# An attention and mixture-of-experts kernel: the first batch's experts computed per chosen pair instead of densely

## The chip, the cores and the metric

The kernel runs as one program on one core of a Trainium2 chip. The time is device time in microseconds (us) of one execution, and a kernel's time is the median of its runs. The engines are called as the profile calls them: PE is TensorE (matrix products), PEld its loads of weights, DVE is VectorE, ACT is ScalarE, POOL is GpSimd, SP is SyncE, which here only starts transfers (DMAs). Each engine works through its own queue of instructions in order, and waits where an operand is not there yet.

## The reference

The input is x, two batches of 1024 tokens of 256 numbers, in float32. A first attention layer with one head (queries, keys and values of 256) is added to x and normalised. A block follows: a layer norm, a causal attention with 16 heads of 128 with rotary embedding, a residual, and a mixture of four experts behind a second layer norm, of which each token uses two:

```python
raw = jax.nn.softmax(x @ w_gate, axis=-1)                  # x: 2048 tokens x 256, 4 experts
top_vals, top_idx = jax.lax.top_k(raw, TOP_K)              # TOP_K = 2
w = jax.nn.softmax(top_vals, axis=-1)
comb = jnp.zeros((t, E), x.dtype).at[jnp.arange(t)[:, None], top_idx].add(w)
hmid = jax.nn.gelu(jnp.einsum('td,edi->tei', x, we1) + be1[None], approximate=False)
eout = jnp.einsum('tei,eid->ted', hmid, we2) + be2[None]   # we1, we2: 4 x 256 x 256
out = jnp.einsum('te,ted->td', comb, eout)
```

The experts' output is added to the block's residual, and a last normalisation gives the result. The reference computes every expert for every token and multiplies by `comb`, in which two of the four weights of each token are zero.

## The kernel before

**Tiles.** A row tile is 128 tokens on the 128 partitions; a batch has eight (`NT`), J0 is tiles 0 to 3 and J1 tiles 4 to 7. An attention row (`RowA`, `RowB`) is the work of one head on one row tile: scores on PE, a mask and row maximum on DVE, an exponential on ACT, a normalisation, a transposition of the probabilities, the product with the values (av), and the output product. For some rows the probabilities are transposed in blocks by DVE and put together by SyncE transfers (`gather`, the pT copies, line 702), for others by PE. There are 272 rows: 16 of the first attention, then 256 of the second in 32 units of eight rows, a unit being one head of one batch. Row `s` = 256 begins the last two units; the loop over rows ends at 272.

**Order.** Nothing is left to a scheduler. `do(f, ...)` writes a named operation down; `at`, `first`, `mid`, `end_of` and `late` attach one to a row's step; `step(t)` writes down the parts of the rows that are under way and what is attached. The list `MOVES` then takes single operations to behind another one, by name, and `ordered` gives the final order in which all of them are issued:

```python
    for f in ordered(ops, MOVES):
        f()
```

**The experts before.** `m_stats`, `m_rstd`, `m_norm` make the second layer norm (`m_norm` of batch 0 on GpSimd, of batch 1 on VectorE, one instruction for a row tile), `m_transposed` (line 524 by its helper) turns it, `gate_products` and `gate_logits` (1626, 1642) make the logits, `gate`, `gate_best`, `gate_weights` (1664 to 1708) find each token's two experts and weights on VectorE with two exponentials on ACT. `m_bias` (1715) adds the weighted second bias. `hidden(b, j, e)` (1728, 1736) is four products of 512 columns for one expert and four tiles, evacuated by ACT with the Gelu; `expert(b, j, slots)` (1751, 1760) is the second product of 256 columns, added with its weight to `h`, the residual, by VectorE. So each batch runs eight hiddens and eight sets of expert products. `m_residual` (1611) adds the residual with accumulating transfers of GpSimd, `o_stats` and `o_finish` make the last normalisation and store it. `load_experts` (1538 to 1544) loads `we1` and `w_gate`; `load_second` (1548 to 1550) `we2` and its bias. Exponential, square root and Gelu need different function tables on ACT; `table()` puts a load of the table in front where the last one was of the Gelu.

Batch 0's layer norm, gate and first two hiddens lie among the last 16 rows. After row 271 come batch 0's other experts, with batch 1's residual, norm and gate between them, and then batch 1's experts:

```python
    do(m_rstd, 1, J0)
    do(m_bias, 0, (3,))
    do(all_of, 0, 0, 1)
    do(m_norm, 1, 0)
```

`all_of(b, j, e)` is `expert` for one expert and four tiles. Products are collected in PSUM: scores in `ps_sc` (two), transposes in `ps_tr` (two), hiddens in `acc_tile()` (two of 512 columns). `rope_sb` holds the rotary tables, last used by the last rotation; `lent` is two tiles that the first attention's weights leave to `we2`; x1 is the first attention's output, held in SBUF until it is stored.

## Time and profile before

| what | value |
|---|---|
| median of three runs | 1139.58 us (1139.5 to 1141.21) |
| the profiled execution's own time | 1144.33 us |
| its span, first to last instruction | 1141.7 us |
| granted PE clock over the span | 0.998 |
| bytes moved by DMA | 133.89 MB, 117 GB/s on average |
| of these from and to device memory | 22.71 MB read, 4.19 MB written |

The profile records one execution. Its page gives each engine's busy time, the chain of work that ended last, and groups of instructions by line and shape. In the trace, one row stands for neighbouring instructions of one kind: start, duration, engine, line, operation, out<-in, shapes and number, and in square brackets how long the engine waited before it and for what. A row of a stretch gives the stretch, its duration, the busy time and number of instructions of PE, PEld, DVE, ACT and POOL, the granted PE clock, the share of DMA time and GB/s. Matrix products in float32 appear as two records each. GpSimd's last rotation ends at 957.9, and the last PE instruction at 1136.0.

### The profile page before, as it was taken

What the parts mean: (1) busy time and instruction counts of PE and PEld (TensorE: products, weight loads), DVE (VectorE), ACT (ScalarE), POOL (GpSimd) and SP (SyncE); (2) the same over time, 40 slices, a digit from 0 to 9 for tenths busy, and PEclk for the clock granted to TensorE, in tenths of its full rate; (3) what the DMA queues carried; (4) which work ended last, traced back from release to release, by engine and by line L of the source; (5) the groups of instructions that cost most, each with busy time, mean ns of one, the idle gap of its engine ahead of it and who ended that gap; (6) DMA issues with size and microseconds to landing.
All of it is one profiled execution on the core that took longest, in us unless ns stands there. A gap on an engine that the chain in (4) does not pass through costs nothing.

```text
span 1141.7 us, 15909 instructions
## 1 busy us (share of the span) xinstructions
PE 1125.4 (99%) x4616; PEld 714.3 (63%) x4616; DVE 782.5 (69%) x1809; ACT 651.9 (57%) x1228; POOL 784.3 (69%) x736
## 2 busy tenths in 40 slices
PE   9999989999999999999999999999999999999998
PEld 6666645656565656565757575757575657566665
DVE  5557776858585867676767676676767678576575
ACT  3333576665656565656565656565656556553444
POOL 4005999999998989697869777888889999000000
PEclk9999999999999999999999999999999999999999
DMA  6132475666556454555555545555555576414311
GB/s 190 38 87 59 118 175 131 154 137 128 127 119 132 114 139 111 120 119 131 118 125 134 126 111 130 129 139 128 135 135 134 125 156 160 108 43 91 58 38 37
DMA packets 243453, 133.89 MB, mean 117 GB/s; under 512 B 18884, under 2 KB 241160, under 8 KB 242856
## 3 DMA queue, kind: packets, MB, share of 16 engines
q1 hardware_dynamic: 238352, 121.45, 46.1%
q0 software_dynamic: 2288, 6.98, 2.7%
q10 hardware_dynamic: 2728, 4.46, 1.1%
q8 instruction: 37, 0.61, 0.2%
q14 instruction: 48, 0.39, 0.1%
HBM read 22.71 MB, written 4.19 MB: 24 GB/s over the span
## 4 chain that ended last, share of the span: by engine, by line
PE 90%; POOL 5%; DVE 2%; ACT 1%; SPq 1%; DMA 1%; issue 0%; ACTq 0%; POOLq 0%; DVEq 0%
PE av L1240 21%; PE sc L1174 20%; PE pa L950 10%; PE pa L941 6%; PE pa L1098 5%; PE pa L1728 5%; PE pe L1751 4%; PE pc L950 4%; PE sc L721 2%; PE pc L1098 2%; PE pc L941 2%; POOL rot L863 2%; PE pa L770 2%; PE pa L611 1%; PE pa L624 1%; PE pa L1050 1%
## 5 line engine op out<-in xcount | busy, mean ns | idle before, releaser
L1191 ACT ACTIVATE pr<-pr,rs 128x128 f32<-128x128 f32 (+3 forms) x252 | 196.0, 779 | 190.5 <-DVE rs L1189 190.3
L643 DVE CUSTOM_DVE_ANT_0 sc<-sc,mask 128x640 f32<-128x640 f32 (+7 forms) x272 | 206.4, 759 | 128.2 <-PE sc L1174 113.5
L1174 PE MATMUL sc<-Twk,Twq 128*128 128x512 f32 (+3 forms) x768 | 289.5, 487 | 2.8 <-ACT pr L651 1.9
L1240 PE MATMUL av<-pT,vg 128*128 128x512 f32 (+3 forms) x768 | 270.0, 489 | 3.6 <-DMA pT<-pair_sb 3.3
L651 ACT ACTIVATE pr<-sc,nmx 128x640 f32<-128x640 f32 (+7 forms) x272 | 201.2, 740 | 114.0 <-DVE nmx L643 86.6
L1240 PEld LDWEIGHTS av<-pT,vg 128*128 128x128 f32 x768 | 143.7, 191 | 127.5 <-issue 100.1
L863 POOL TENSOR_TENSOR rot<-Twk,rope_sb 64x512 f32<-64x512 f32 x128 | 166.5, 1301 | 79.1 <-DVE Twk L983 57.5
L1174 PEld LDWEIGHTS sc<-Twk,Twq 128*128 128x128 f32 x768 | 135.6, 191 | 123.0 <-issue 104.0
L863 POOL TENSOR_TENSOR rot<-Twq,rope_sb 64x512 f32<-64x512 f32 x128 | 169.1, 1321 | 8.8
L691 DVE STREAM_TRANSPOSE x<-pr 128x640 f32<-128x640 f32 (+1 forms) x124 | 128.6, 1038 | 20.4 <-ACT pr L1191 17.7
L865 POOL TENSOR_TENSOR Twk<-Twk,rot 128x512 f32<-128x512 f32 x64 | 87.0, 1359 | 5.0
L864 POOL TENSOR_TENSOR Twk<-Twk,rope_sb 128x512 f32<-128x512 f32 x64 | 85.6, 1337 | 5.0
L864 POOL TENSOR_TENSOR Twq<-Twq,rope_sb 128x512 f32<-128x512 f32 x64 | 82.4, 1288 | 5.0
L865 POOL TENSOR_TENSOR Twq<-Twq,rot 128x512 f32<-128x512 f32 x64 | 82.1, 1283 | 5.0
L691 DVE STREAM_TRANSPOSE pair_sb<-pr 128x128 f32<-128x128 f32 (+1 forms) x120 | 60.5, 504 | 11.6 <-ACT pr L1191 11.5
L1611 POOL DMA_DIRECT2D hx<-x_dram x4 | 3.5, 1145 | 91.5 <-DVE hx L1715 82.4
L1107 DVE TENSOR_TENSOR hx<-hx,pa 128x512 f32<-128x512 f32 x70 | 48.0, 686 | 22.2 <-PE pa L1098 21.2
L1256 ACT ACTIVATE aT_sb<-av,par 128x512 f32<-128x512 f32 x64 | 43.9, 687 | 30.9 <-PE av L1240 26.3
L1728 PE MATMUL pa<-xT,we_flat 128*128 128x512 f32 x128 | 57.5, 593 | 0.0
L1751 PE MATMUL pe<-lent,hT 128*128 128x256 f32 x240 | 54.4, 379 | 0.0
L651 ACT ACTIVATION_READ_ACCUMULATOR pr<-sc,nmx 128x1 f32 x272 | 53.4, 196 | 0.0
L1751 PEld LDWEIGHTS pe<-lent,hT 128*128 128x128 f32 x240 | 45.4, 190 | 9.5 <-issue 3.1
(221 smaller groups left out, 1794.6 us busy)
## 6 DMA issues: line engine op xcount, KB each, us to landing
pT<-x SPq DMA_DIRECT2D x496, 128.0 KB, 2.7
pT<-pair_sb SPq DMA_DIRECT2D x480, 64.0 KB, 2.0
pT<-aT_sb SPq DMA_DIRECT2D x48, 128.0 KB, 2.6
pT<-za SPq DMA_DIRECT2D x48, 64.0 KB, 2.0
wk_g<-in_L_ffn_wk_dram SPq DMA_DIRECT2D x9, 256.0 KB, 3.0
wq_g<-in_L_ffn_wq_dram SPq DMA_DIRECT2D x9, 256.0 KB, 3.1
wv_g<-in_L_ffn_wv_dram SPq DMA_DIRECT2D x9, 256.0 KB, 3.0
wo_g<-in_L_ffn_wo_dram SPq DMA_DIRECT2D x9, 256.0 KB, 2.9
```

Of the source, the lines that this page charges most:

```text
L643: nc.vector.tensor_tensor_reduce(out=sc[:, :L], in0=sc[:, :L], in1=mask[:, S - L :], scale=-1.0, scalar=BIG, op0=ALU.add, op1=ALU.min, acc ...
L651: nc.scalar.activation(pr[:, :L], sc[:, :L], AF.Exp, bias=nmx, scale=-1.0, accum_out=sm)
L691: nc.vector.transpose(z[:, i % 4, :n, :], pr[:, : n * 32].rearrange("p (m s) -> p m s", s=32))
L863: nc.gpsimd.tensor_tensor(rot[lo, :], t[hi, cs], rope_sb[hi, 1, cs], ALU.mult)
L864: eng.tensor_tensor(t[:, cs], t[:, cs], rope_sb[:, 0, cs], ALU.mult)
L865: nc.gpsimd.tensor_tensor(t[:, cs], t[:, cs], rot, ALU.add)
L950: nc.tensor.matmul(pa, lhsT=w, rhs=x, start=start, stop=True, skip_group_check=True)
L1174: nc.tensor.matmul(sc[:, ds(n0, n)], lhsT=qT[:, ts(i, P)], rhs=kT[:, ds(n0, n)], start=True, stop=True,)
L1191: nc.scalar.activation(self.pr[:, :L], self.pr[:, :L], AF.Copy, scale=rs)
L1240: nc.tensor.matmul(cut(av), lhsT=vg[g, b][:, c, ts(hh, HD)], rhs=cut(pT[:, c, :]), start=(c == 0), stop=(c == i),)
L1728: nc.tensor.matmul(ph, lhsT=we1_sb[:, e, c, ts(m, P)], rhs=x2T[:, c, ds(k0 * P, 512)], start=(c == 0), stop=(c == DC - 1),)
L1751: nc.tensor.matmul(pe[:, ts(n, D)], lhsT=hTs[b, j, e][:, c, ts(k, P)], rhs=we2_sb[e][:, c, :], start=(c == 0), stop=(c == IC - 1),)
```

## The change

Batch 0's eight hiddens and eight sets of expert products are taken out. In their place:

- The gate is made some rows earlier, and `m_norm` of batch 0 moves from GpSimd to VectorE. `ws` keeps the two weights of each token.
- Each (token, expert) pair chosen gets a slot. Slots are grouped by expert, each expert beginning a new tile of 128; with 2 x 8 tiles of pairs and at most three more for the rounding up, there are `NS` = 19 slot tiles. `sparse_counts` counts tokens per expert by two products with constant matrices; `sparse_slots` turns the counts into each pair's slot (`place_ids`) and each slot tile's expert (`expert_ids`). Constants and small tables lie in the rotary table's space, written by `sparse_constants` after the last rotation.
- `sparse_scatter` writes each normalised row to its two slots in device memory (`slot_x`), with 16 indirect DMAs of GpSimd, a memset behind each. `slot_x` is filled with zeros by seven DMAs on SyncE near the start. `sparse_load` reads the slots back, four tiles a DMA.
- Per slot tile, `sparse_transposed`, `sparse_hidden` and `sparse_out` compute one expert: w1 is copied within SBUF by SyncE from an address in a register (`sparse_weights`), w2 is read by PE at an address in a register, and each register is loaded from `expert_ids` (`sparse_ids`). Results go to `slot_y` in device memory, two tiles a store.
- `sparse_gather` reads both results of each token back into x1's space with 16 indirect DMAs of GpSimd, and `sparse_add` adds them with their weights on VectorE, 16 instructions.
- `PLACES` attaches the first part to the last 16 rows; `queue` and `MORE` set how many slot operations stand between the parts of batch 1's work after row 271. Batch 1's experts stay dense. Of `MOVES`, 49 entries at the end of the list go and seven come.

```diff
--- before.py
+++ after.py
 MOVES = (
     ("m_rstd 1 7", "o_finish 1 1 2"),
-    ("o_finish 1 1 1", "o_stats 1 1 2"),
...
-    ("m_stats 0 0.1.2.3", "load_experts"),
+    ("o_finish 1 1 1", "expert 1 1 3.3"),
+    ("o_finish 1 1 0", "expert 1 1 3.2"),
+    ("hidden 1 1 2", "o_finish 0 1 0.1.2.3"),
+    ("hidden 1 0 2", "sparse_add 0 3"),
+    ("RowB.transpose 271", "b_output 7 1 2.3"),
+    ("RowB.scores 266", "RowB.gather 263 0"),
+    ("b_output 6 1 3", "RowB.transpose 263"),
     ("load_weights 6 wo #2", "RowB.normalise 254"),
...
+    lent_flat = const.tile([P, B * 3 * 512], F32, name="lent")
+    lent = [lent_flat[:, ts(b, 3 * 512)] for b in range(B)]
...
+    NS = 2 * NT + E - 1
+    slot_x = dpool.tile([NS * P, D], F32, name="slot_x")
+    slot_y = dpool.tile([NS * P, D], F32, name="slot_y")
...
+    for k in range(0, NS, 3):
+        n = min(3, NS - k)
+        nc.sync.dma_start(
+            slot_x[ds(k * P, n * P), :].rearrange("(n p) d -> p n d", p=P),
+            mask[:, : n * D].rearrange("p (n d) -> p n d", d=D),
+        )
...
-                nc.vector if b else nc.gpsimd,
+                nc.vector,
...
+    def sparse_constants():
+        g = nc.gpsimd
+        g.memset(ones, 1.0)
+        g.memset(before, 1.0)
+        g.affine_select(
+            out=before, in_=before, compare_op=ALU.is_ge, fill=0.0, base=-1,
+            pattern=[[1, P]], channel_multiplier=-1,
+        )
+        for k in range(NT):
+            g.memset(limits[:, :, k : k + 1], float(k * P))
+        for n in range(NS):
+            g.memset(starts[:, n, :], float(n * P))
+        for t in steps_of:
+            g.memset(t[:, :NT, :], 0.0)
+        g.memset(steps_of[0][:, NT : NT + 1, :], 0.0)
+        g.memset(tiles_of[:, 0, :], 0.0)
+        g.memset(marks[:, :, 0:1], 1.0)
+        g.memset(marks[:, :, E : E + 1], 0.0)
...
+    def sparse_counts(b):
+        nc.vector.tensor_tensor(picked, found[b, 0][1], found[b, 1][1], ALU.add)
+        pc = ps_tr.tile([P, 512], F32, tag="tr", name="pc")
+        flat = picked.rearrange("p t e -> p (t e)")
+        for k, lhsT in enumerate((ones, before)):
+            nc.tensor.matmul(
+                pc[:, ts(k, NT * E)], lhsT=lhsT, rhs=flat, start=True, stop=True
+            )
+        counts[b] = pc
+    def sparse_slots(b):
...
+        v.tensor_copy(place_ids, places)
+        v.tensor_tensor(
+            marks[:, :, 1:E], starts,
+            bases[:, 1:].unsqueeze(1).to_broadcast([P, NS, E - 1]), ALU.is_ge,
+        )
+        v.tensor_reduce(experts_of, marks[:, :, 1:E], AX.X, ALU.add)
+        v.tensor_copy(expert_ids, experts_of)
...
+    def sparse_scatter(b, t):
+        for n in range(2):
+            put = nc.gpsimd.indirect_dma_start(
+                out=slot_x, out_offset=at_row(n, t),
+                in_=xn2[b, t // 4][:, t % 4, :], in_offset=None,
+            )
+            tc.declare_no_dep(put.ins, group="slots", reason="each slot is of one token and choice")
+            tc.add_to_no_dep_group("slots", put.ins)
+            puts.append(put.ins)
+            nc.gpsimd.memset(ones[:, 0:1], 1.0)
+    def sparse_ids(engine, lo, hi):
+        _, vals = nc.values_load_multi_w_load_instructions(
+            expert_ids[0:1, lo:hi], engines=[engine], min_val=0, max_val=E - 1,
...
+    def sparse_load(k):
+        n = min(4, NS - 4 * k)
+        tag = ("Twk", "Twk", "Twq")[k % 3]
+        t = bpool.tile([P, 4, D], F32, tag=tag, name="xs", bufs=BUFS[tag[1:]])
+        nc.sync.dma_start(
+            t[:, :n, :], slot_x[ds(4 * k * P, n * P), :].rearrange("(n p) d -> p n d", p=P)
+        )
+    we1_rows = we1_flat.rearrange("p (e x) -> p e x", e=E)
+    we2_rows = lent_flat[:, : E * IC * D].rearrange("p (e x) -> p e x", e=E)
+    def sparse_weights(s):
+        t = wpool.tile([P, DC, I], F32, tag=("wq", "wk", "wv")[s % 3], name="w1")
+        nc.sync.dma_start(
+            t.rearrange("p c i -> p (c i)"),
+            we1_rows[:, ds(sp_ids[s], 1), :].rearrange("p a x -> p (a x)"),
+        )
+    def sparse_transposed(q):
+        n = min(2, NS - 2 * q)
+        pt = ps_tr.tile([P, 512], F32, tag="tr", name="pt")
+        for k in range(n):
+            for c in range(DC):
+                nc.tensor.transpose(
+                    pt[:, ds(c * 256 + k * P, P)], x_slots[2 * q + k][:, ts(c, P)], ident
+                )
+        t = pools["l"].tile([P, 512], F32, tag="part", name="xT_s", bufs=2)
+        for c in range(DC):
+            w = par[:, cols["ln2_w"] + c : cols["ln2_w"] + c + 1]
+            bc = par[:, cols["ln2_b"] + c : cols["ln2_b"] + c + 1]
+            dst, src = t[:, ds(c * 256, n * P)], pt[:, ds(c * 256, n * P)]
+            if c % 2:
+                nc.vector.tensor_scalar(dst, src, w, bc, ALU.mult, ALU.add)
+            else:
+                nc.scalar.activation(dst, src, AF.Identity, bias=bc, scale=w)
+        xT_slots[q] = t
+    h_ring, h_slots = [], {}
+    def sparse_hidden(s):
+        if not h_ring:
+            t = bpool.tile([P, 512], F32, tag="rot", name="h_s", bufs=1)
+            h_ring.extend((t[:, :256], t[:, 256:], bo_sb))
+        q, k = divmod(s, 2)
+        ph = acc_tile()
+        for m in range(IC):
+            for c in range(DC):
+                nc.tensor.matmul(
+                    ph[:, ts(m, P)],
+                    lhsT=w_slots[s][:, c, ts(m, P)],
+                    rhs=xT_slots[q][:, ds(c * 256 + k * P, P)],
+                    start=(c == 0),
+                    stop=(c == DC - 1),
+                )
+        t = h_ring[s % len(h_ring)]
+        for m in range(IC):
+            nc.scalar.activation(
+                t[:, ts(m, P)], ph[:, ts(m, P)], AF.Gelu,
+                bias=biases[:, s, m : m + 1],
+            )
+        other.append(s)
+        h_slots[s] = t
+    def sparse_out(s):
+        q, k = divmod(s, 2)
+        n = min(2, NS - 2 * q)
+        pe = acc_tile()
+        for c in range(IC):
+            nc.tensor.matmul(
+                pe[:, :D],
+                lhsT=h_slots[s][:, ts(c, P)],
+                rhs=we2_rows[:, ds(pe_ids[s], 1), ts(c, D)].rearrange("p a d -> p (a d)"),
+                start=(c == 0),
+                stop=(c == IC - 1),
+            )
+        evacuate(y_ring[q % 2][:, ts(k, D)], pe[:, :D])
+        if k + 1 == n:
+            y = y_ring[q % 2][:, : n * D]
+            nc.sync.dma_start(
+                slot_y[ds(2 * q * P, n * P), :].rearrange("(n p) d -> p n d", p=P),
+                y.rearrange("p (n d) -> p n d", d=D),
+            )
+    def sparse_gather(t):
+        for n in range(2):
+            nc.gpsimd.indirect_dma_start(
+                out=x1[:, 2 * t + n, :], out_offset=None, in_=slot_y, in_offset=at_row(n, t)
+            )
+    def sparse_add(b, t):
+        for n in range(2):
+            hb = h[:, b * NT + t, :]
+            nc.vector.scalar_tensor_tensor(
+                hb, x1[:, 2 * t + n, :], ws[b][n][:, t : t + 1], hb, ALU.mult, ALU.add
+            )
...
+    at(s - 2, sparse_constants)
+    PLACES = (
+        (0, "at", m_stats, 0, J0),
+        (0, "at", m_rstd, 0, J0),
+        (0, "end", m_norm, 0, 0),
+        (2, "end", m_stats, 0, J1),
+        (3, "at", m_rstd, 0, J1),
+        (3, "at", m_norm, 0, 1),
+        (2, "first", m_transposed, 0, 0, 0),
+        (4, "first", m_transposed, 0, 0, 1),
+        (5, "first", m_transposed, 0, 1, 0),
+        (6, "first", m_transposed, 0, 1, 1),
+        (6, "at", gate_products, 0),
+        (7, "at", gate_logits, 0),
+        (8, "first", gate, 0),
+        (8, "at", gate_best, 0, 0),
+        (8, "at", gate_best, 0, 1),
+        (9, "mid", sparse_counts, 0),
+        (9, "end", sparse_slots, 0),
+        (11, "at", sparse_scatter, 0, 0),
+        (11, "at", sparse_scatter, 0, 1),
+        (13, "at", sparse_scatter, 0, 2),
+        (13, "at", sparse_scatter, 0, 3),
+        (14, "at", sparse_scatter, 0, 4),
+        (12, "at", sparse_scatter, 0, 5),
+        (13, "at", sparse_scatter, 0, 6),
+        (13, "at", sparse_scatter, 0, 7),
+        (10, "at", sparse_ids, SP, 0, 3),
+        (13, "at", gate_weights, 0),
+        (10, "at", sparse_biases),
+        (11, "at", sparse_weights, 0),
+        (11, "at", sparse_weights, 1),
+        (11, "at", sparse_weights, 2),
+        (14, "at", sparse_load, 0),
+        (14, "at", sparse_load, 1),
+        (16, "at", sparse_load, 2),
+        (17, "at", sparse_transposed, 0),
+        (17, "mid", sparse_hidden, 0),
+        (18, "at", sparse_hidden, 1),
+    )
...
+    queue = deque()
+    for n in range(NS + 1):
+        if 2 <= n < NS:
+            queue.append((sparse_hidden, n))
+        if n:
+            if n + 2 < NS:
+                queue.append((sparse_ids, SP, n + 2, n + 3))
+                queue.append((sparse_weights, n + 2))
+            queue.append((sparse_ids, PE, n - 1, n))
+            queue.append((sparse_out, n - 1))
+            if n % 2 and n // 2 < NT:
+                queue.append((m_bias, 0, (n // 2,)))
+        if n % 2 == 0 and n + 2 < NS:
+            queue.append((sparse_transposed, n // 2 + 1))
+        if n in (4, 8):
+            queue.append((sparse_load, 2 + n // 4))
+    MORE = deque((0, 1, 3, 5, 7, 4, 4, 0, 5, 99))
+    def more():
+        n = MORE.popleft()
+        while n > 0 and queue:
+            f, *args = queue.popleft()
+            do(f, *args)
+            n -= f in (sparse_hidden, sparse_out)
     step(end)
-    for i in (0, 2):
-        do(b_output, G - 1, 1, (i, i + 1))
+    do(b_output, G - 1, 1, (0, 1))
+    more()
+    do(b_output, G - 1, 1, (2, 3))
     do(m_stats, 1, J0)
-    at(end + 1, all_of, 0, 0, 0)
     step(end + 1)
-    at(end + 2, hidden, 0, 0, 2)
+    more()
     step(end + 2)
     do(m_rstd, 1, J0)
-    do(m_bias, 0, (3,))
-    do(all_of, 0, 0, 1)
     do(m_norm, 1, 0)
-    do(m_bias, 0, (4, 5))
-    do(hidden, 0, 0, 3)
+    more()
     for c in range(DC):
         do(m_transposed, 1, 0, c)
-    do(all_of, 0, 0, 2)
-    do(hidden, 0, 1, 0)
-    do(all_of, 0, 0, 3)
+    more()
     do(steps[end - 1].output, END)
-    do(m_bias, 0, (6, 7))
-    do(hidden, 0, 1, 1)
+    more()
     for i in (4, 6):
         do(b_output, G - 1, 1, (i, i + 1))
     do(m_residual, 0, J0)
     do(m_residual, 1, J0)
     do(m_residual, 0, J1)
     do(m_stats, 1, J1)
-    do(all_of, 0, 1, 0)
-    do(o_stats, 0, 0, J0)
-    do(hidden, 0, 1, 2)
     do(m_rstd, 1, J1)
-    do(m_rstd, 0, J0)
     do(m_norm, 1, 1)
-    do(all_of, 0, 1, 1)
     do(m_residual, 1, J1)
+    more()
     for c in range(DC):
         do(m_transposed, 1, 1, c)
-    do(hidden, 0, 1, 3)
+    more()
     do(gate_products, 1)
     do(gate_logits, 1)
+    more()
     do(gate, 1)
     do(gate_best, 1, 0)
     do(gate_best, 1, 1)
-    do(all_of, 0, 1, 2)
+    more()
     do(gate_weights, 1)
+    more()
+    for t in range(NT):
+        do(sparse_gather, t)
     do(hidden, 1, 0, 0)
-    do(all_of, 0, 1, 3)
+    do(m_bias, 1, (0, 1))
     do(hidden, 1, 0, 1)
-    do(m_bias, 1, (0, 1))
-    do(o_finish, 0, 0, J0)
     do(all_of, 1, 0, 0)
-    do(o_stats, 0, 1, J0)
+    do(m_bias, 1, (2, 3))
     do(hidden, 1, 0, 2)
-    do(m_rstd, 0, J1)
     do(all_of, 1, 0, 1)
-    do(o_finish, 0, 1, J0)
-    do(m_bias, 1, (2, 3))
+    for t in J0:
+        do(sparse_add, 0, t)
     do(hidden, 1, 0, 3)
+    do(o_stats, 0, 0, J0)
+    do(m_rstd, 0, J0)
     do(all_of, 1, 0, 2)
     do(m_bias, 1, (4, 5))
     do(hidden, 1, 1, 0)
+    for t in J1:
+        do(sparse_add, 0, t)
+    do(o_finish, 0, 0, J0)
     do(all_of, 1, 0, 3)
+    do(o_stats, 0, 1, J0)
     do(hidden, 1, 1, 1)
+    do(m_rstd, 0, J1)
     do(o_stats, 1, 0, J0)
     do(m_rstd, 1, J0)
     do(all_of, 1, 1, 0)
+    do(o_finish, 0, 1, J0)
     do(hidden, 1, 1, 2)
     do(m_bias, 1, (6, 7))
     do(all_of, 1, 1, 1)
```

## The prediction

> **What bounds the kernel now.** I read first the page's busy times and chain, then TensorE by shape, then the stretches around the changed work, then the orders of TensorE, ScalarE, GpSimd and SyncE there.
>
> ```profile
> PE 1125.4 (99%) x4616; PEld 714.3 (63%) x4616; DVE 782.5 (69%) x1809; ACT 651.9 (57%) x1228; POOL 784.3 (69%) x736
> ...
> PE 90%; POOL 5%; DVE 2%; ACT 1%; SPq 1%; DMA 1%; issue 0%; ACTq 0%; POOLq 0%; DVEq 0%
> ```
>
> TensorE bounds everything, so the change is worth what it takes off TensorE less the waits it puts there. By stretch (duration, then busy time of PE, PEld, DVE, ACT, POOL, the granted clock, DMA):
>
> ```profile
> 951.00:979.00 28.00, 27.60 (x127) 17.98 (x126) 18.66 (x53) 18.74 (x37) 17.51 (x19) 1.00 0.71 167
> 979.00:1010.00 31.00, 28.62 (x115) 17.11 (x114) 21.28 (x68) 17.93 (x34) 0.00 (x0) 0.94 0.47 111
> 1010.00:1136.00 126.00, 126.00 (x473) 84.72 (x471) 80.97 (x220) 56.20 (x84) 3.55 (x4) 1.00 0.21 46
> ```
>
> From 1010 on, where nearly all expert work lies, TensorE never waits. In the last two attention units (951 to 1010) it waits 2.8 us, mostly once, and that costs clock too:
>
> ```profile
> 990.21 0.38 PE L1642 MATMUL pt<-ident,logitT 128*128 128x128 f32 x2
> 992.61 3.92 PE L1240 MATMUL av<-pT,vg 128*128 128x512 f32 x8 [2.02 <-DMA pT<-pair_sb]
> ```
>
> Eight such records take 2.16 us elsewhere; these took 3.92, the granted clock being 0.66 from 992 to 996: a 2.02 us wait cost 1.7 us more.
>
> **TensorE's own work.** Each f32 matmul is two records, and start-to-start spacing gives the prices:
>
> ```profile
> 938.73 1.06 PE L1098 MATMUL pc<-we_flat 128*128 128x128 f32 x8
> 939.62 1.46 PE L1174 MATMUL sc<-Twk,Twq 128*128 128x512 f32 x4
> ...
> 967.13 0.60 PE L524 MATMUL pt<-ident,xn 128*128 128x128 f32 x4
> 967.57 1.67 PE L1174 MATMUL sc<-Twk,Twq 128*128 128x512 f32 x4
> ...
> 1061.26 3.60 PE L1728 MATMUL pa<-xT,we_flat 128*128 128x512 f32 x8
> 1064.69 3.62 PE L1751 MATMUL pe<-lent,hT 128*128 128x256 f32 x16
> 1068.15 1.04 PE L524 MATMUL pt<-ident,pair_sb 128*128 128x128 f32 x8
> ```
>
> 128 columns: 0.89/8 = 0.111 us a record; a transpose 0.44/4 = 0.11; 512 columns 3.43/8 = 0.429; 256 columns 3.46/16 = 0.216. Removed: batch 0's eight hidden calls and eight expert sets, 8 x 3.43 + 8 x 3.46 = 55.1. Added per slot tile: two transposes 0.22, a hidden of 8 records 0.89, an output of 4 records 0.86; 19 x 1.97 = 37.4. **Net -17.7 us**, counts included; all on the path. No slot is fewer: 19 tiles are computed whatever the tokens choose.
>
> **Waits that go.** The 2.8 us above and 1.7 of clock: **-4.5**; that place gets waits of its own now.
>
> **Before the scatter.** sparse_constants puts about 38 small GpSimd instructions between the last rotation (ends 957.9) and the gate's memset, which SyncE's w_gate load and then the 16 pT copies of row 255 wait for. Memsets of 128x128 take 0.20, four small ones 0.21 together: some 2.3 us. GpSimd loses m_norm (9.69 us) to VectorE, 8 x 0.41 = 3.3 there, under its idle time (9.3 of 28 us). The copies move to 960.8-971.3 and land about 974.5; TensorE asks at 973.3: 1.5 us. VectorE is in order: its x1 transpose waits for that landing, and behind it stand row 263's softmax, the gate (15 operations at 0.22, as in the row below), two row steps and the one-hot sum. I put that sum at 985.6; TensorE reaches the counts at 982.9 and everything behind is held: 2.8 us. The TensorLoad on SyncE then stands between the two halves of row 263's copies (0.66 us an issue) and holds the second half until the slots are known: 1.0 us at row 263's av. **+5.3** (0 if gate and copies keep their lead, 9 if each slips as far again).
>
> **Scatter and load.** After the counts VectorE needs a b_output addition, a 1.2 us transpose, a softmax start and 17 small operations at 0.2: place ids at about 992.4. Then 16 indirect DMAs leave GpSimd one by one. None is in the trace; its DMA rows are
>
> ```profile
> 967.60 0.78 POOL L1548 DMA_DIRECT2D lent<-in_L_ffn_we_dram  x1
> 968.38 0.58 POOL L1550 DMA_DIRECT2D lent<-in_L_ffn_be_dram  x1
> ...
> L1611 POOL DMA_DIRECT2D hx<-x_dram x4 | 3.5, 1145 | 91.5 <-DVE hx L1715 82.4 <-DVE pair_sb L518 9.0
> ```
>
> Bounds: 0.6 (plain) and 2.0 (a row list costing the gap 0.6 to 1.3 of a whole 128x512 pass again). I take 1.15, the dearest DMA row, since each row needs its own address; with the memset behind it 1.25. The last is issued at 992.4 + 15 x 1.25 = 1011.2; GpSimd's 256 KB loads land after 5.3 us and its 1 KB ones after 4.3, so 1016; SyncE's slot loads wait for all 16, and 512 KB lands some 4.5 us later (256 KB 4.5, 512 KB 6.3 at the crowded start): 1020.6. TensorE, which no longer has batch 0's first two hiddens, is at the first slot transpose at 1013.6. **+7.0**; at 0.6 us a DMA the wait is gone, at 2.0 it is 20.
>
> **The slot loop.** A dense hidden has seven buffers and two score banks to run ahead with; the slots alternate between two banks of one 512-column tile. A hidden cannot start until the Gelu two places before has read its bank. So what holds ScalarE holds TensorE. Before, the gate of batch 1 held it like this:
>
> ```profile
> 1077.99 1.28 ACT L1581 ACT_TABLE_LOAD   x1
> 1079.29 0.23 ACT L1668 ACTIVATE raw_g<-lg 128x32 f32<-128x32 f32 x1
> 1082.78 0.21 ACT L1695 ACTIVATE e<-e 128x8 f32<-128x8 f32 x1 [3.26 <-DVE e L1693]
> 1083.01 1.28 ACT L1736 ACT_TABLE_LOAD   x1
> ```
>
> That is 6.3 us, and TensorE had 6.9 us of expert work queued (1077.3 to 1084.2). Now the same gate stands between slots 13 and 15: with the logits ahead and the evacuation and Gelu behind, ScalarE is late by 9.1 us from the gate's products, and TensorE has 1.0 + 0.2 + 0.87 + 0.89 + 0.87 + 0.44 = 4.3 to do: 4.8. Likewise batch 1's two rstd pairs (1.28 + 0.5 + 1.28): behind slot 1, with the first table load (1.28, which waits for the first hidden), 5.0; behind slot 9, where the additions and statistics of four tiles come first, 3.0. **+12.8** (bounds 4 and 20: the table loads may be partly early, or VectorE's m_bias, 2 us each, may stand in front).
>
> Each output starts with a TensorLoad, in order on TensorE's sequencer, after the hidden it was to run behind. No row shows one: 0 if queued work covers it, at most a small DMA's round trip, 1.7. From the middle, 0.85, I take off the lead the sequencer gains on a hidden, 0.4 (the gate's records leave every 0.06 us, a hidden's run 0.111): 0.45 for the 13 slots outside the waits above, **+5.9** (0 to 25). The Trainium skill's DMA: Bandwidth & Descriptors, Latency and other measured facts, gives a floor of about 0.6 us for a tensor load. By it this term would be an estimated 2.6, the forecast 1150.
>
> SyncE's 256 KB weight copy (3.0) has three buffers and about 6 us: hidden, half a microsecond at slot-output stores if not.
>
> **Clock.** Waits of 2.8, 7, 5, 3 and 4.8: by the one row (2.02 us wait, 1.7 lost), three of them count, the others share a window. **+5.1** (0 to 9). The Trainium skill, TensorE: Matmul & The Clock Gate, section 1, says that only an idle window of about 3.4 us halves the clock. The 2.02 us above speaks against taking that as a threshold for a wait. By the page two or three of these waits would count, an estimated 4.
>
> **At nothing.** The seven zero fills: SyncE issues nothing between 6.7 and 42.0, and 2.4 MB at the 190 GB/s of the first slice is 13 us. The merged lent: names only. The 16 gathers and 16 additions: GpSimd is idle (0.00 busy after 1064), the first eight take about 3 + 10 + 4 us against 14 to 17 us of dense work; uncovered they stop VectorE, not yet TensorE (at 2.0 us each some 8). VectorE loses 32 additions of 0.48 and gains 16. The reordered end and dropped moves: 0 to 1; the last addition, statistics and store stay.
>
> Sum: -17.7 - 4.5 + 5.3 + 7.0 + 12.8 + 5.9 + 5.1 = +13.9. The profiled execution took 1144.33 (span 1141.7 and 2.6 around it), 4.75 above the median of 1139.58; I add the sum to the median: **1153**.
>
> **Rivals.**
> *The loop keeps TensorE's pace.* The 4616 records already run through two alternating banks without waits, and queued LDWEIGHTS run ahead. Then the 18.7 of the loop and two clock losses (3.4) vanish: 1131. It decides at 13.9 us of loop and clock waits saved. Against: one slot has 1.97 us of TensorE, where the covered stop was 6.3.
> *Indirect DMAs at 2.0 us.* Wait of 20 instead of 7, plus 8 at the gathers: 1153 + 21 = 1174. For: one by one on one queue; against: plain ones at 0.6.
> *Scatter in time.* At 0.6 us the 7.0 and one clock loss go: 1144, still slower.
> *The change does less than it says:* no; the removed calls are gone from the program.
>
> **Numbers.** Forecast and scatter in time together 0.52 (1142 to 1166), loop at pace 0.26, dear DMAs 0.19, a cancellation within 0.2% (2.3 us, about what the three runs can tell) 0.03. Range 1129 to 1178: loop at pace with 2 off, dear DMAs with 4 on. The slower cases alone: 1142 to 1178. Faster 0.27, same 0.04, slower 0.69.
>
> **What would show it.** TensorE busy total down by some 17; a wait on a DMA of xs at the first slot transposes; idle before slot matmuls put down to ACT; indirect rows on GpSimd near 1.15; clock below 1 in several windows after 985. Wrong if a slot takes 2.0 us throughout, or if the slots are loaded before 1013.

## The result, and the profile after

The changed kernel takes 1157.17 us (median of four runs, 1155.96 to 1159.16) against 1140.39 for the kernel before: a ratio of 1.0148, 95% interval 1.0127 to 1.0169. That is 16.8 us more by the medians, where 13.9 were forecast; the time lies inside the range of 1129 to 1178. The profiled execution took 1155.96 us, its span 1154.3.

The page's first line, busy time and instructions by engine:

```profile
PE 1116.3 (97%) x4694; PEld 717.2 (62%) x4694; DVE 793.4 (69%) x1844; ACT 651.3 (56%) x1263; POOL 808.9 (70%) x814
```

TensorE is busy for 9.1 us less, and the span is 12.6 us longer: its idle time (span less busy) rose from 16.3 to 38.0, by 21.7. The chain of waits says nothing this time: it breaks off within the last microseconds. The stretches do; duration, busy time of PE, PEld, DVE, ACT, POOL, the granted clock, DMA share, GB/s:

```profile
951.00:979.00 28.00, 24.81 (x125) 16.49 (x125) 23.72 (x57) 15.12 (x33) 8.97 (x47) 0.94 0.70 177
979.00:1010.00 31.00, 25.67 (x96) 15.80 (x95) 23.05 (x89) 13.26 (x29) 12.31 (x23) 1.00 0.58 156
1010.00:1060.00 50.00, 44.38 (x225) 34.62 (x223) 23.52 (x54) 22.82 (x45) 7.96 (x13) 0.93 0.72 185
1060.00:1100.00 40.00, 29.69 (x162) 22.31 (x162) 22.86 (x68) 17.19 (x39) 2.90 (x3) 0.96 0.47 136
1100.00:1160.00 60.00, 48.85 (x178) 33.26 (x176) 40.58 (x111) 26.04 (x47) 13.35 (x14) 0.98 0.22 68
```

Every stretch up to 1100 has lost TensorE time: 3.2, 5.3, 5.6 and 10.3 us, 24.4 in all, where before the same part had 2.8. The last one, batch 1's dense experts, still runs without a wait. What ended the waits from 900 on (total us, number, longest):

```profile
PE pa L1929 <- DMA w<-we_flat: 4.8, 1, 4.8
PE pa L1950 <- ACT rope_sb L474: 4.3, 2, 2.5
PE pt L496 <- DVE xn L490: 3.1, 3, 1.3
PE pa L1929 <- ACT bo_sb L1938: 2.1, 2, 1.7
PE pc L1794 <- DVE rope_sb L1790: 2.1, 1, 2.1
PE av L1212 <- issue: 1.6, 1, 1.6
PE pt L1905 <- DMA xs<-slot_x: 1.6, 1, 1.6
PE pa L1022 <- DVE hx L1032: 1.1, 1, 1.1
```

There is no one wait that costs 17 us. Three places need a closer look.

**The normalisations on VectorE.** In the timeline (start, duration, engine, line, number), four instructions of one form take 5.22 us the first time (row tiles 0 to 3) and 1.38 the second (tiles 4 to 7). The rows with x1 show the second to fourth of the first time singly:

```profile
953.96 5.22 DVE L490 TENSOR_SCALAR xn<-hx,mvh,rsh 128x256 f32<-128x256 f32 x4
...
954.46 1.43 DVE L490 TENSOR_SCALAR xn<-hx,mvh,rsh 128x256 f32<-128x256 f32 x1
955.81 1.70 DVE L490 TENSOR_SCALAR xn<-hx,mvh,rsh 128x256 f32<-128x256 f32 x1
957.43 1.75 DVE L490 TENSOR_SCALAR xn<-hx,mvh,rsh 128x256 f32<-128x256 f32 x1
...
965.59 1.38 DVE L490 TENSOR_SCALAR xn<-hx,mvh,rsh 128x256 f32<-128x256 f32 x4 [0.62 <-ACT rsh L487]
...
954.47 1.27 POOL L836 TENSOR_TENSOR Twq<-Twq,rope_sb 128x512 f32<-128x512 f32 x1
955.81 1.26 POOL L837 TENSOR_TENSOR Twq<-Twq,rot 128x512 f32<-128x512 f32 x1
...
957.92 0.65 POOL L1778 MEMSET rope_sb<- 128x3 f32 x19
...
959.23 0.47 PE L496 MATMUL pt<-ident,xn 128*128 128x128 f32 x1 [1.34 <-DVE xn L490]
```

The second normalisation starts at 954.46 and the third at 955.81, each with a rotation product of GpSimd, and each outlasts it (the third runs on into the constants); the fourth ends at 959.18, just after the block of constants. TensorE's transposes wait three times behind them. The Trainium skill, SBUF — State Buffer, Who interferes with whom, has the rule: VectorE and GpSimd share a port pair, and a `tensor_scalar` of VectorE in a two-port mode waits for the whole GpSimd instruction that holds it. These rows agree with it: 1.43 us beside GpSimd's 1.27, 0.35 each without. In which mode they ran, no row says.

**The scatter.** First and last indirect DMA, the slots' loads on SyncE, the first transposes:

```profile
995.59 1.08 POOL L1856 DMA_INDIRECT slot_x<-xn,rope_sb  x1 [23.95 <-DVE rope_sb L1828]
...
1014.92 0.96 POOL L1856 DMA_INDIRECT slot_x<-xn,rope_sb  x1 [0.19 <-issue]
...
1017.34 1.47 SPq L1883 DMA_DIRECT2D xs<-slot_x  x3
...
1021.32 0.63 PE L1905 MATMUL pt<-ident,xs 128*128 128x128 f32 x4 [1.59 <-DMA xs<-slot_x]
```

From first to last are 19.3 us, 1.29 each. TensorE came at 1019.7 and waited only 1.6 us, because it had already lost 8.5 before.

**The late copy.** One copy of w1, issued at 1056.3, held TensorE for 4.8 us from 1063.6. The first row below is the issue of the residual's accumulating transfers (a fourth followed at 1063), the last two are the transfers between 1040 and 1075 (number, size, median us to landing):

```profile
1053.25 2.73 POOL L1583 DMA_DIRECT2D hx<-x_dram  x3 [37.25 <-DVE hx L1688]
...
1056.29 2.87 SPq L1894 DMA_DIRECT2D w<-we_flat  x2
...
1068.40 1.83 PE L1929 MATMUL pa<-xT_s,w 128*128 128x128 f32 x7 [4.80 <-DMA w<-we_flat]
...
w<-we_flat SPq DMA_DIRECT2D x8, 256.0 KB, 3.4
hx<-x_dram POOLq DMA_DIRECT2D x4, 512.0 KB, 9.1
```

The slowest copy took 11.9 us to land, the quickest 2.3; the DMA engines were busy all the time from 1059 to 1068.

**The clock.** Inside the stretches above, the granted clock is 0.68 and 0.75 from 958 to 964, 0.66, 0.50 and 0.70 from 1023 to 1032 and 0.79 and 0.78 from 1066 to 1074 (by 3 or 4 us), so it fell behind the normalisations, at the first slots and at the late copy. That sums to 6.9 us lost.

### The profile page after: what moved, and what is told of

Read it like the earlier page. It is cut to its first block, busy times and chain, and to the rows that moved or that the text cites. A ratio compares the mean times of both kernels' runs of the same rounds, so it can differ in the third digit from the quotient of the medians.

```text
span 1154.3 us, 16450 instructions
## 1 busy us (share of the span) xinstructions
PE 1116.3 (97%) x4694; PEld 717.2 (62%) x4694; DVE 793.4 (69%) x1844; ACT 651.3 (56%) x1263; POOL 808.9 (70%) x814
## 5 line engine op out<-in xcount | busy, mean ns | idle before, releaser
L955 DVE TENSOR_TENSOR Twq<-pa,part 128x512 f32<-128x512 f32 x30 | 20.5, 682 | 41.3 <-PE pa L922 41.3
L913 PEld LDWEIGHTS pa<-wv_g,xT 128*128 128x128 f32 x360 | 44.6, 192 | 5.8 <-issue 5.5
L947 ACT ACTIVATE part<-pa,par 128x512 f32<-128x512 f32 x60 | 41.0, 683 | 12.0 <-PE pa L922 12.0
```

The source lines that it names most:

```text
L913: nc.tensor.matmul(pa[:, ts(n, P)], lhsT=x[:, ts(n, P)], rhs=w, start=start and n == 0, stop=True, skip_group_check=True,)
```

## The experiments

My first theory was that the waits listed are costs that add, so that taking one away gains its length. The rival: something behind each of them is due nearly as late, so that single mendings gain nothing. All ratios below are to the kernel before, run beside it, with 95% intervals. The intervals of e1 to e7 and of e10 overlap with the changed kernel's, so their small differences in time can't be told from noise; e8, e9 and e12 are clearly quicker than it. e2, e3, e5, e6, e8, e9 and e12 leave out something that the result needs, and serve only to measure it.

| run | time, us | ratio to before |
|---|---|---|
| changed kernel | 1157.17 | 1.0148 [1.0127, 1.0169] |
| e1 normalisation on ScalarE | 1156.42 | 1.0142 [1.0124, 1.0159] |
| e2 fixed w1 | 1157.18 | 1.0143 [1.0126, 1.0160] |
| e3 fixed w2 | 1157.51 | 1.0159 [1.0133, 1.0185] |
| e4 residual apart | 1159.41 | 1.0164 [1.0144, 1.0184] |
| e5 e1 and half the scatter | 1154.89 | 1.0121 [1.0104, 1.0137] |
| e6 e2 and e4 | 1154.96 | 1.0128 [1.0111, 1.0145] |
| e7 first reciprocal deviation early | 1156.16 | 1.0146 [1.0127, 1.0165] |
| e8 all of these | 1146.74 | 1.0054 [1.0037, 1.0072] |
| e9 e8, no table loads in the loop | 1145.88 | 1.0044 [1.0030, 1.0057] |
| e10 mended, nothing left out | 1153.60 | 1.0116 [1.0088, 1.0144] |
| e12 e8 with the full scatter | 1148.58 | 1.0071 [1.0054, 1.0088] |

**e1: the first four normalisations on ScalarE.**

```diff
+        if not b and not j:
+            nb = small.tile([P, 4], F32, tag="nbo", name="nb")
+            nc.vector.scalar_tensor_tensor(
+                nb, mv_h[b][:, cs, 0], -1.0, rstd_h[b][:, cs], ALU.mult, ALU.mult
+            )
...
+            if not b and not j:
+                nc.scalar.activation(
+                    xn[:, k, :], ht, AF.Identity,
+                    bias=nb[:, k : k + 1], scale=rstd_h[b][:, i : i + 1],
+                )
+                continue
             ln_apply(
```

> The first four normalisations of batch 0 are made by ScalarE (four Identity activations with scale and bias, one small VectorE product for the bias) in place of VectorE. My theory: on VectorE these four took 5.2 us, as each waited for the GpSimd instruction then running (two rotation products of 1.27 us and the block of constants), where the other four took 1.38; so the 3.1 us of TensorE waits at the transposes of xn and the clock lost behind them (granted 0.75 and 0.91 for 10 us, about 1.7) vanish, and the rows' VectorE work, the gate and the scatter come some 3 to 5 us earlier with them. Time: 3 to 6 us less than the changed kernel, 1151 to 1154. Rival: the stop is not on the path that counts, the slots' data come from a chain of their own; then the wait at the first slot transposes (now 1.6 us) grows by what TensorE gains, and the time stays within 1.5 us of 1157.

Measured: 1156.42, 0.75 less. The waits at the transposes of xn fell from 3.1 to 0.9 us, as the theory says, but the time went to the rival. TensorE's waits in e1, from 950 on:

```profile
PE pt L1917 <- DMA xs<-slot_x: 2.8, 1, 2.8
...
PE av L1212 <- DMA pT<-pair_sb: 1.7, 1, 1.7
...
PE pt L496 <- ACT xn L1581: 0.9, 4, 0.4
```

The first slot transposes start at 1020.9 instead of 1021.3, and what TensorE gained ahead of them it waits for the slots' data and for a row's copies. (In e1 the line numbers behind the edit are 12 higher.)

**e2: w1 of a fixed expert, without copies.**

```diff
-        t = wpool.tile([P, DC, I], F32, tag=("wq", "wk", "wv")[s % 3], name="w1")
-        nc.sync.dma_start(
-            t.rearrange("p c i -> p (c i)"),
-            we1_rows[:, ds(sp_ids[s], 1), :].rearrange("p a x -> p (a x)"),
-        )
-        w_slots[s] = t
+        w_slots[s] = we1_sb[:, s % E]
```

> The slots take w1 of a fixed expert (slot number modulo 4) straight from its resident tile: the 19 copies of 256 KB and their register loads on SyncE are gone. Theory: the 4.8 us wait at 1063 to 1068 is a copy that took 11.9 us to land because four accumulating transfers of 512 KB filled the DMA engines; but VectorE stands until 1067.5 for the last of the same transfers, and behind it the evacuations, so without the copies TensorE stops about 2 us later instead: 2 to 4 us less than the changed kernel, 1153 to 1155. Rival a: the late copy alone is the cause; then 5 to 7 us less (4.8 and the clock behind it), 1150 to 1152. Rival b: the register loads on SyncE, which hold row 263's copies (1.6 us wait before the last av), matter too; then another 1 to 2 us less.

Measured: 1157.18, nothing gained. The 4.8 us are gone, and in their place (the profiled execution is the slowest of four, 1159.02):

```profile
PE pt L496 <- DVE xT_s L1909: 5.7, 2, 5.1
...
PE pt L1900 <- DMA xs<-slot_x: 3.4, 1, 3.4
```

VectorE stands at the weighted bias of row tile 4 for the accumulating transfer into the same tile, with an evacuation behind it, and TensorE waits 5.1 us for that. My reading of the place was right, but "about 2 us later" was too little.

**e3: w2 of a fixed expert, no register loads on TensorE.**

```diff
-                rhs=we2_rows[:, ds(pe_ids[s], 1), ts(c, D)].rearrange("p a d -> p (a d)"),
+                rhs=we2_rows[:, s % E, ts(c, D)],
```

> The slots take w2 of a fixed expert (slot number modulo 4) by a fixed address: the 19 register loads on TensorE are gone, everything else stays. Theory: they cost TensorE next to nothing, since its sequencer runs ahead: 0 to 3 us less than the changed kernel (the slot loop has about 3 us of gaps that no wait explains), 1154 to 1157. Rival, the prediction's term: 0.45 us a slot for 13 slots, 5.9 us less, 1151.

Measured: 1157.51, no gain. The changed kernel's trace shows the loads themselves (min/median/max ns):

```profile
L1869 PEldq TENSOR_LOAD <-rope_sb x19: 295/311/1809, 1023.3 to 1091.2; - x19
```

0.31 us in the median, in the sequencer, beside products that are already queued. TensorE's waits there ahead of an output product that nothing else explains come to 0.2 us, where the prediction's 0.45 for each of 13 slots makes 5.9. But the loads are not always free: in e6 one took 1.26 us, another 1.24, and TensorE waited 0.8 us at each of the two output products that read their registers:

```profile
L1869 PEldq TENSOR_LOAD <-rope_sb x1: 1257/1257/1257, 1037.1 to 1037.1; - x1
...
1038.57 0.69 PE L1945 MATMUL pa<-lent,bo_sb 128*128 x2 [0.82 <-issue]
...
PE pa L1945 <- issue: 1.6, 2, 0.8
```

**e4: the accumulating transfers taken apart.**

```diff
     do(m_norm, 1, 0)
+    do(m_residual, 1, J0)
...
-    do(m_residual, 0, J0)
-    do(m_residual, 1, J0)
-    do(m_residual, 0, J1)
     do(m_stats, 1, J1)
...
+    do(m_residual, 0, J0)
+    do(m_residual, 0, J1)
     for t in range(NT):
         do(sparse_gather, t)
```

> The four accumulating transfers of the residual are taken apart: batch 1's first right behind its normalisation, batch 0's two behind the last slot and ahead of the gathers; batch 1's second stays. Theory: both the copy of w1 that took 11.9 us to land and VectorE's 4.4 us wait for the transfer come from their standing together; the 4.8 us wait of TensorE and the clock behind it (0.55 for 3 us) go: 5 to 7 us less than the changed kernel, 1150 to 1152. Rival: the transfers only move and meet the slot loop's loads and copies elsewhere, or hold up the gathers and the additions at the end: within 2 us of 1157.

Measured: 1159.41, if anything longer. VectorE no longer waits for a transfer, but copies of w1 still came late twice (1.3 us at 1041, 2.8 at 1073): the first transfer now fell among the slots' loads and the last rows' copies, and GpSimd sent two others at 1065.8 and 1066.4.

**e5: e1 and half the scatter.**

```diff
     def sparse_scatter(b, t):
-        for n in range(2):
+        for n in range(1):
```

> As e1 (first four normalisations on ScalarE), and only each token's first choice is scattered: 8 indirect DMAs in place of 16, the other slots keep their zeros; everything behind computes the same amount. Theory: the first slot transposes began at 1020 to 1021 in the changed kernel and in all four runs so far, whatever TensorE did before, because the slots' data arrive then (ids at 995, 16 DMAs of 1.27 us, landing and load); so TensorE's gains before it were lost. With 8 DMAs the data are there near 1011, TensorE starts the slots when it comes, at 1018 or before: 3 to 6 us less than e1, 1150 to 1154. Rival: SyncE's order or the DMA engines hold the loads, not the number of indirect DMAs: first slot transpose still at 1020 or later, within 1.5 us of 1156.4.

Measured: 1154.89, 1.5 less than e1, half of the least expected. The scatter did hold the slots: with 8 DMAs the loads left at 1008.0 instead of e1's 1016.9, and TensorE began the slots without a wait at 1018.2. But it then waited 1.8 us for VectorE's evacuation of that transpose, 4.9 for a copy, and 3.9 at a row's copies at 973 to 977 (1.7 in e1). That last wait lies ahead of the scatter, where e5 is the same as e1.

**e6: the diffs of e2 and e4 together.**

> e2 and e4 in one: fixed w1 without copies, and the accumulating transfers taken apart. Alone, neither gained. Theory: in the slot loop each had the other behind it: without the copies TensorE waited 5.1 us for VectorE, which stood for an accumulating transfer, and with the transfers apart the copies still came late (4.1 us) behind other loads. Without both, 5 to 8 us less than the changed kernel, 1149 to 1152. Rival: a third wait takes over again (ScalarE's table loads, the evacuations), and the time is again 1155 or more.

Measured: 1154.96, 2.2 less, where 5 to 8 were expected. Both waits are gone, but the slots' data cost 3.5 us instead of 1.6, a row's copies at 977 2.2 instead of nothing, the register loads 1.6 (above), and the gate's and the deviation's 4.4 stayed.

**e7: batch 1's first reciprocal deviation early.**

```diff
     end = len(steps)
+    at(end + 1, m_rstd, 1, J0)
+    at(end + 1, m_norm, 1, 0)
     for t in range(end):
...
-    do(m_rstd, 1, J0)
-    do(m_norm, 1, 0)
```

> Batch 1's first reciprocal deviation and normalisation stand ahead of the first slot's hidden, so before the first Gelu: two table loads on ScalarE (2.56 us) leave the slot loop, nothing is left out. Theory: the waits of 1.7 us and 0.6 us behind them (at 1034 and 1036) go, with a part of the clock loss: 2 to 4 us less, 1153 to 1155. Rival: ScalarE was not the last thing there, the copies of w1 and the transfers catch up: within 1.5 us of 1157.

Measured: 1156.16, 1.0 less. The waits behind the first deviation's table loads are gone, and those for copies of w1 rose from 4.8 (one) to 8.6 us (three).

So seven edits gave +2.2 to -2.3 us, though all but e3 and e4 took away the wait that they aimed at. In the traces of e1, e2 and e7 another wait grew in its place, which is the rival. One reservation: each trace is one execution, and executions differ without an edit. Up to 977 the engines' orders in e4, e6 and e7 are the changed kernel's, yet at the normalisations and at the row's copies behind them TensorE waited 3.1 and 0 us there, 1.5 and 2.6 in e4, 2.3 and 2.2 in e6, 1.8 and 2.4 in e7.

**e8: all of it together**, the diffs of e2, e3, e4, e5 (with e1) and e7.

> All of it together: normalisation on ScalarE, half the scatter, fixed w1 and w2 (no copies, no register loads), transfers apart, the first reciprocal deviation early. The number of matrix products is the changed kernel's. Theory: the prediction's price of the products is right (17.7 us less than before) and the rest is waits and the clock behind them; left are the counts (2.1), the evacuation and the first Gelu (1.6), the second reciprocal deviation (1.8), the gate (3.7) and some 5 us of clock: 1136 to 1143, about the time of the kernel before. Rival: the slots' products themselves cost more than 1.97 us each, as small products and their weight loads do not keep the pace: above 1147 with few waits in the profile.

Measured: 1146.74, 10.4 us less than the changed kernel. That is more than the single runs together (e3, e5, e6 and e7 sum to -5.2, though with an uncertainty of 2 to 3 us each), but 3.7 above the top of what I expected, and still 0.5% slower than before. In e8 TensorE's waits from 950 on are

```profile
PE pa L1957 <- ACT rope_sb L474: 4.8, 2, 3.0
PE pc L1806 <- DVE rope_sb L1802: 2.1, 1, 2.1
PE pa L1936 <- DVE xT_s L1921: 1.8, 1, 1.8
```

and thirteen other causes of 0.2 to 1.4: 17.8 us in all. Its busy time is 1113.4, not the 1107.7 of the price. The rival, that slots cost more than 1.97 us each, does not explain this: the rows of the changed kernel show that price wherever TensorE doesn't stop (below). What stands above the price is waits and the clock behind them.

**e9: no table loads in the loop.** The gate's exponential becomes (1 + t) / (1 - t), with t the hyperbolic tangent of half the argument:

```diff
+            nc.scalar.activation(raw, lg, AF.Tanh, scale=0.5)
+            nc.vector.tensor_scalar(den, raw, -1.0, 1.0, ALU.mult, ALU.add)
+            nc.vector.reciprocal(den, den)
+            nc.vector.scalar_tensor_tensor(raw, raw, 1.0, den, ALU.add, ALU.mult)
...
-    do(m_rstd, 1, J1)
+    do(m_rstd_v, 1, J1)
```

`m_rstd_v` is one VectorE reciprocal.

> e8, and ScalarE loads no function table inside the slot loop: batch 1's gate takes its exponentials from the hyperbolic tangent, which lies in the Gelu's table, and batch 1's second reciprocal deviation is replaced by VectorE's reciprocal of the variance (the root is left out). Theory: of the 17.8 us of TensorE waits left in e8, 4.8 stand behind an evacuation that ScalarE gave late for these two; they go, with the clock behind them (2.07 us for eight products that take 1.06): 4 to 7 us less than e8, 1140 to 1143. Rival: VectorE, which has three more operations in the gate and orders the evacuations, holds TensorE as long; then 1145 or more.

Measured: 1145.88, 0.9 less than e8. Between the first Gelu and batch 1's dense experts no table is loaded, and the gate's wait is still there. ScalarE in e9:

```profile
1069.55 0.21 ACT L1691 ACTIVATE e<-e 128x8 f32<-128x8 f32 x1 [4.09 <-DVE e L1689]
1069.67 0.35 ACT L474 COPY rope_sb<-pa 128x256 f32<-128x256 f32 x1
```

ScalarE works in order. The slot's evacuation stands behind the gate's second activation, which waits 4.1 us for VectorE's chain of small operations; TensorE waits 3.8 us for the bank (3.0 in e8). e9 alone can't separate the two causes, as its gate has three more VectorE operations in that chain. The changed kernel's own trace does:

```profile
1076.71 1.28 ACT L1553 ACT_TABLE_LOAD   x1
1078.73 0.23 ACT L1640 ACTIVATE raw_g<-lg 128x32 f32<-128x32 f32 x1 [0.74 <-DVE lg L1637]
1082.21 0.21 ACT L1667 ACTIVATE e<-e 128x8 f32<-128x8 f32 x1 [3.25 <-DVE e L1665]
1082.32 0.35 ACT L474 COPY rope_sb<-pa 128x256 f32<-128x256 f32 x1
1082.69 1.28 ACT L1938 ACT_TABLE_LOAD   x1
```

The first table load is done 0.74 us before VectorE delivers the logits, and the evacuation that TensorE waits for ends as the second load begins. At the gate the table loads were beside the point.

**e10: mended, with nothing left out**: e1, e4, e7, the tangent of e9, and this:

```diff
         if k + 1 == n:
             y = y_ring[q % 2][:, : n * D]
-            nc.sync.dma_start(
+            nc.gpsimd.dma_start(
                 slot_y[ds(2 * q * P, n * P), :].rearrange("(n p) d -> p n d", p=P),
```

> Nothing left out: the changed kernel with the first four normalisations on ScalarE, batch 1's first reciprocal deviation ahead of the first Gelu, the gate of batch 1 by the hyperbolic tangent, the accumulating transfers apart, and the slots' results stored by GpSimd's queue, so that SyncE's copies of w1 don't stand behind a store that waits for an evacuation. The scatter, the copies and the second reciprocal deviation stay. Theory: the slots begin at 1020 to 1021 as in e1, the loop loses some 8 us of waits and clock: 1147 to 1151, still 7 to 11 above the kernel before. Rival: the copies still come late or the stores now do, as each single mending so far has found another wait: 1153 or more.

Measured: 1153.60, 3.6 less than the changed kernel and short of what I expected. One copy of w1 still costs 3.3 us (it left SyncE at 1032.7, behind eight copies of a row, and the DMA engines were busy from 1018 to 1040), the gate 3.1, the slots' data 2.1. So the accumulating transfers are not the only thing that makes a copy late. No version here beats the kernel before.

**e11: the kernel before, a second profile**, without an edit.

> The kernel before once more, for a second profile: the profiled execution shown took 4.75 us more than its median. Theory: nothing of it lies in the stretches compared, from 950 to the end; TensorE takes 185 us from there to its last product, with 3 us of waits, and the surplus lies ahead of it. Rival: the stretch behind 950 itself was slow in the profile shown (its 2.02 us wait and the clock behind it); then it is 3 us shorter here.

Measured: 1138.66, span 1136.5. The same wait as in the prediction's profile, in both rows 2.02 us:

```profile
989.15 2.39 PE L1240 MATMUL av<-pT,vg 128*128 128x512 f32 x8 [2.02 <-DMA pT<-pair_sb]
```

The eight products behind it took 2.39 us, not 3.92, and the granted clock of that stretch is 1.00, not 0.94. Theory and rival each hold in part: the same products are reached 3.45 us earlier (947.98 against 951.43), so most of the surplus lies ahead of 950, and 1.5 us lie in this place.

**e12: e8 with `range(2)` again in `sparse_scatter`.**

> e8 with the full scatter of 16 indirect DMAs, all other edits of e8 kept: the scatter's price where nothing else covers it. In e8 TensorE reached the slots at 1016.1 and did not wait. Theory: with 16 DMAs the last is issued near 1014, the slots' data are there at 1019.5 to 1020.5 as in the runs with 16, and 3.4 to 4.4 us of wait at the first slot transposes come back, with up to 2 of clock, and go through to the end: 1150 to 1153. Rival: a later wait absorbs them again, as it did with each single mending, and the time stays at 1146 to 1148.

Measured: 1148.58, 1.8 more than e8; the intervals of the ratios overlap. The wait at the slots came back as worked out, 3.4 us, first slot at 1019.2. Part of it was taken in by the next wait: the 1.8 us for VectorE's evacuation in e8 are not there in e12.

## Why the prediction was right, step by step

The direction and the size are right, and so is the main mechanism: the products saved are outweighed by waits that the small steps bring. That the sum comes as near as 13.9 to 16.8 is partly luck, as its terms were wrong both ways. Against e11, a cleaner profile of before, the changed kernel's span is 17.8 us longer: TensorE's idle time rose by 23.2 (14.8 to 38.0), its busy time fell by 5.4.

- **TensorE's own work, -17.7.** The price holds. Where TensorE doesn't stop, the changed kernel's slots show it:

```profile
1047.44 1.06 PE L1929 MATMUL pa<-xT_s,w 128*128 128x128 f32 x8
1048.34 1.03 PE L1950 MATMUL pa<-lent,bo_sb 128*128 x4
1049.20 0.60 PE L1905 MATMUL pt<-ident,xs 128*128 128x128 f32 x4
1049.64 1.06 PE L1929 MATMUL pa<-xT_s,w 128*128 128x128 f32 x8
```

From start to start, a hidden takes 0.90, an output 0.86 and the transposes of two slots 0.44: 1.98 a slot. Busy time fell by 9.1 all the same (5.4 against e11), not by the 17 that the prediction named as a sign. Against e11, the granted clock, 0.994 to 1.000, is 6.9 us of 1154, which TensorE spends on the same products. That leaves 5.4. I put some 3 of it to the ends of groups: the four transposes above are busy for 0.60 where the next group starts after 0.44, and ahead of each stop these 0.16 us count as busy; from 940 on the changed kernel has some 20 stops, e11 three. No row names the rest.
- **Waits that go, -4.5.** The 2.8 us were right. The 1.7 of clock is not in every execution: e11 has the same wait without it. Adding the sum to the median rather than to the profiled time was therefore the right choice, but the term was too large.
- **Before the scatter, +5.3.** The counts cost 2.1 (2.8 forecast) and row 263's copies 1.6 (1.0; the profile names no releaser for this wait). Row 255's copies, put at 1.5 (974.5 less 973.3 makes 1.2), cost nothing in this execution, and e4, e6 and e7 had 2.2 to 2.6 at a row's copies near there. Missed is the step that was costed at nothing, "8 x 0.41 = 3.3 there, under its idle time": the normalisations took 5.2 us for the first four, and TensorE waited 3.1. The cover named was VectorE's idle time; what they needed was GpSimd's. A `b_output` addition behind the slot arithmetic cost 1.1 more.
- **Scatter and load, +7.0.** The DMA was taken as 1.25 us with its memset and measured 1.29; the ids were there at 995.3 instead of 992.4, the slots began at 1021.3 instead of 1020.6. The rival with 2.0 us a DMA falls with that. The wait itself was 1.6, since TensorE was late by its own waits. The two terms together, 12.3, met 10.1.
- **The slot loop, +12.8.** The waits put down to ScalarE come to 8.0 us in the loop: 3.3 at the first slots, 1.8 at the second reciprocal deviation, 2.9 at the gate; VectorE adds 1.3. The mechanism was right (an in-order ScalarE holds two banks), the sizes some 60% too high (5.0, 3.0 and 4.8 were forecast). At the gate the chain on VectorE makes the wait, not the table loads, as the rows under e9 show.
- **Register loads, +5.9.** Wrong in size: e3 shows no gain without them, and the changed kernel's trace has 0.2 us of TensorE waits that may be theirs. e3 alone would not prove it, since another wait can cover a gain, and e6 shows that a slow load does stop TensorE (1.6 us in all). The page cited, DMA: Bandwidth & Descriptors, Latency and other measured facts, has a floor of some 0.6 us for a load; here the median is 0.31.
- **The copies, "hidden".** Wrong: one wait of 4.8 us. Three buffers ahead were not enough while the DMA engines were full; that the four transfers of 512 KB alone filled them is not shown, as copies came late in e4 and e10 too, with the transfers apart. By luck it stands in for the register loads in the sum.
- **Clock, +5.1.** 6.9 by the mean clock. In this execution, waits of 2.1 at the counts and 2.5 at the gate cost no clock, and the normalisations, which the forecast had at nothing, did.
- **The rivals.** "Scatter in time" had 0.6 us a DMA as its condition, and 1.29 were measured; the wait at the slots was a mere 1.6 all the same, without its 1144: the waits lay elsewhere. "The loop keeps TensorE's pace" had 0.26. Even e9, which leaves out most of what it could lack, takes 1145.88, 15 above its 1131.

What failed in the method is the adding. The terms were priced one by one as if independent; in e1, e2 and e7 a wait taken away was largely waited for elsewhere, so a single term of 3 to 6 us can be wrong with little effect on the time.

## What to carry to other kernels

Cutting TensorE's work into small steps that pass through ScalarE, VectorE, a register and a DMA each, in place of long products with deep buffers, can cost a wait at each place where another engine's queue is in order; here products priced at 17.7 us were saved, and TensorE's idle time rose by 21.7. When an operation is moved to an engine, look at what its neighbours run at that moment, not only at its own idle time. Expect little from removing one wait where several stand close behind each other: remove them together, or read what is due next. And compare single traces with care: a wait can move by 2 us between executions ahead of any edit.

## What the hardware showed that I had not expected

- A VectorE normalisation of 128x256 takes 0.35 us alone, 1.43 beside a GpSimd product of 1.27, and 1.75 beside its block of memsets. The trace of before shows single ones of up to 1.43 us at 65 to 145, where the rotations run: it could have been read.
- A wait of 2.02 us lost 1.5 us of clock in one execution and none in another. The Trainium skill, TensorE: Matmul & The Clock Gate, What's actually happening, tells of a free-running window of 3.4 us, which fits that it depends on the moment; that the window must be idle as a whole doesn't fit the execution that lost it.
- An indirect DMA of 128 rows of 1 KB holds GpSimd for 0.97 us and the next scatter follows after 1.27 to 1.29 with a memset between, a gather, without a memset, mostly after 1.25. If scatter and gather are alike in this, the memset costs next to nothing.
- A copy of 256 KB inside SBUF landed after 2.3 us, and after 11.9 beside four accumulating transfers of 512 KB.
- A register load on TensorE's queue takes 0.31 us in the median of 19, but up to 1.81, and in e6 two of 1.26 and 1.24 stopped TensorE for 0.8 each.
